# Second half of the tokens read transposed from memory, ScalarE copying operands of VectorE's sums to PSUM, and the rms factor moved to position 111

## The chip, the cores and the metric

The kernel runs on one core of a Trainium2 chip. A core has a matrix engine (TensorE, PE in the profile), a vector engine (VectorE, DVE), a scalar engine (ScalarE, ACT), GpSimd (POOL) and SyncE (SP), which here only issues DMAs. They run side by side and wait for each other by semaphores. The metric is the time of one execution on the device, in microseconds (us), lower is better. Everything is fp32.

## The reference

For x of 2048 tokens by 512 features:

```python
xn = layernorm(x)                                  # no weights
s  = xn @ (weight * block_mask).T                  # 512 x 512, 32x32 blocks kept or zeroed
nx = xn * rsqrt(mean(xn**2) + eps) * ln_w
g, u = nx @ gate_w.T, nx @ up_w.T                  # 1792 x 512 each
ffn = (silu(g) * u) @ down_w.T                     # 512 x 1792
out = x + s * silu(ffn)
```

## The kernel before

**Layout.** Activations are held transposed: features over the 128 partitions, tokens along the free axis, in tiles of 512 tokens. There are four token tiles (t = 0 to 3) and four chunks of features (c = 0 to 3), so the transposed xn is sixteen tiles of 128 x 512. Tokens 0 to 1023 (t = 0, 1) are the first half, t = 2, 3 the second.

**Fewer products.** Both levels of every matrix product use a scheme with seven block products in place of eight. It needs sums and differences of the operands' blocks. On the activations' side, the outer level (`outer_b`) makes four difference tiles (q = 5, 6, 7, 4) for each k and n out of blocks of both halves; the inner level (`inner_b`) makes four more (m = 5, 6, 7, 4) for each outer q. Outer blocks q = 1, 2 are tiles of the first half alone, 3 is the second half's own. The products run with q = 1 and 2 for all eight groups of weights first, and only then with q = 6, 5, 7, 3, 4, so that the second half has the first part of the run to be got ready.

**An order written out by hand.** The kernel calls no scheduler. `at(pos, fn)` records a step under a position, the steps are sorted by position, and this order is the order of each engine's queue. One position is one product of 128x128 with 128x512 on PE. An engine works strictly through its queue: an instruction that waits holds up all behind it. An instance j of seven products has its products at 7j, 7j+2, 7j+3, 7j+4, 7j+6, 7j+8 and 7j+12. Its "seed" at 7j+1 is a copy on ScalarE of the sum x so far into the bank z, which the product at 7j+3 then adds to; its "snapshots" s5 (7j+3) and s2 (7j+5) and its totals are on VectorE or ScalarE.

**PSUM.** Of eight banks, tag "V" has two, used in turn for transposes, for silu's results, for weights scaled on ScalarE and for small things. A third use waits until the first is read.

**The steps that the change touches.**

- `load_x` loads token-major x. `stats` takes mean and variance by token on VectorE, `factors` makes scale and bias from them (with a square root on ScalarE), `normalise` applies these on VectorE or ScalarE, `transpose` turns 128x128 blocks by PE (L155), and `evacuate` copies the banks to SBUF on ScalarE (L163). In the second half the blocks of c = 0 and 1 are not copied: VectorE's outer sums 5 and 7 read them from the bank (positions 51.5 to 74).
- `outer_b` 5, 6, 7 run on VectorE, 4 on GpSimd; `inner_b` 5, 6 on VectorE, 7, 4 on GpSimd. All go through the helper `add`, L97 in the profile.
- `rms_factor` makes the per-token rms factor at 36.2 to 37.4; `rms_store` (position 120) transposes it and stores it to memory, from where it is broadcast over the partitions near the end.
- GpSimd also makes the weights' sums (`inner_a`, also L97), at positions 7 below the instance that uses them.
- `x_t` is the transposed x in memory, read before only at the end, for the residual.

Of the kernel before, what the change touches and what calls it, by code (L numbers as in the profile page):

```python
# [8 lines left out]
F32 = mybir.dt.float32  # L9
I32 = mybir.dt.int32  # L10
AF = mybir.ActivationFunctionType
ALU = mybir.AluOpType
AX = mybir.AxisListType

P = 128
W = 512
# [15 lines left out]
def tile_masked_linear_gated_ffn(  # L32
# [11 lines left out]
    nc = tc.nc  # L44
    NT, H = x.shape
    KC = H // P
    G = gu.shape[0]
    NTT = NT // W
    TT = W // P
# [2 lines left out]
    h_dram = tc.dram_tile([7, G, 2, P, W], F32, name="h_dram")  # L52
    s_dram = tc.dram_tile([KC, NTT, P, W], F32, name="s_dram")
    rms_dram = tc.dram_tile([NT], F32, name="rms_dram")
    acc_dram = tc.dram_tile([G + 1, P, 4, W], F32, name="acc_dram")
    dw_dram = tc.dram_tile([4, P, G, 256], F32, name="dw_dram")

    const = ctx.enter_context(tc.tile_pool(name="const", bufs=1))
    small = ctx.enter_context(tc.tile_pool(name="small", bufs=2))
# [8 lines left out]
    def at(pos, fn, *args):  # L68
        events.append((pos, len(events), fn, args))
# [5 lines left out]
    mem = big.tile([P, sum(n for _, n in RINGS), W], F32, tag="mem", name="mem")  # L75
# [5 lines left out]
    F = first_slot  # L81

    def slot(tag, name=None):
        i, n = ring[tag]
        ring[tag][0] += 1
        return mem[:, first_slot[tag] + i % n, :]
# [6 lines left out]
    def bank(tag, name):  # L93
        return ps.tile([P, W], F32, tag=tag, name=name, bufs=PSB[tag])

    def add(eng, o, a, b, op=ALU.add):
        eng.tensor_tensor(o, a, b, op)  # L97

    dve, pool, act = nc.vector, nc.gpsimd, nc.scalar
# [3 lines left out]
    ident = const.tile([P, P], F32, tag="ident", name="ident")  # L103
# [9 lines left out]

    xt, raw, stat = {}, {}, {}
    agg = small.tile([P, NTT, TT, 2], F32, tag="agg", name="agg", bufs=1)
    rms = small.tile([P, NTT, TT], F32, tag="rms", name="rms", bufs=1)

    def load_x(t):
# [9 lines left out]
    def factors(t):  # L128


        scl = small.tile([P, TT], F32, tag="scl", name=f"scl_{t}")
        nb = small.tile([P, TT], F32, tag="nb", name=f"nb_{t}")
        stat[t] = (scl, nb)

        def last():
            nc.vector.reciprocal(scl, scl)
            nc.vector.scalar_tensor_tensor(nb, agg[:, t, :, 0], -1.0, scl, ALU.mult, ALU.mult)

        return [lambda: nc.vector.tensor_scalar(scl, agg[:, t, :, 1], 1.0 + EPS, EPS * EPS, ALU.mult, ALU.add),
                lambda: nc.scalar.activation(scl, scl, AF.Sqrt), last]  # L140
# [9 lines left out]
    pt = {}  # L150
# [17 lines left out]
    def rms_factor():  # L168

        def first():  # L170
            nc.vector.tensor_scalar_add(rms, agg[:, :, :, 1], EPS)
            nc.vector.reciprocal(rms, rms)
            nc.vector.tensor_mul(rms, agg[:, :, :, 1], rms)
            nc.vector.tensor_scalar_add(rms, rms, EPS)
        return [first, lambda: nc.scalar.activation(rms, rms, AF.Sqrt)]

    def rms_store():

        b = bank("V", "rms_rows")
        nc.tensor.transpose(b[: NTT * TT, :P], rms.rearrange("p t i -> p (t i)"), ident)  # L180
        rows = small.tile([NTT * TT, P], F32, tag="rms_rows", name="rms_rows", bufs=1)
        nc.vector.tensor_copy(rows, b[: NTT * TT, :P])
        nc.sync.dma_start(rms_dram.rearrange("(i p) -> i p", p=P), rows)

# [4 lines left out]
        nc.sync.dma_start(rms_bc[t], rms_dram[t * W : (t + 1) * W].unsqueeze(0).to_broadcast([P, W]))  # L189


    bblk, bop = {}, {}

    def outer_b(q, k, n, eng):


        B = lambda K, H_: pt[2 + n, k] if (K, H_) == (0, 1) else raw[2 * K + k, 2 * H_ + n]
        if q in (1, 2, 3):
            bblk[q, k, n] = B(*{1: (0, 0), 2: (1, 0), 3: (1, 1)}[q])
            return  # L200
        o = mem[:, F["free"], :] if (q, k, n) == (4, 0, 1) else slot("tmp" if (k, n) == (0, 1) else f"B{q}")
        a, b = {
            5: lambda: (B(0, 1), B(0, 0)),
            6: lambda: (B(1, 1), bblk[5, k, n]),
            7: lambda: (B(1, 1), B(0, 1)),
            4: lambda: (B(1, 0), bblk[6, k, n]),
        }[q]()
        add(eng, o, a, b, ALU.subtract)
        bblk[q, k, n] = o

    def inner_b(q, m, eng):

        b11, b12, b21, b22 = (bblk.get((q, k, n)) for k in (0, 1) for n in (0, 1))
        if q in (1, 2):
            b11, b21, b22 = (raw.get((2 * (q - 1) + k, n)) for k, n in ((0, 0), (1, 0), (1, 1)))
        o = slot(f"B{q}", f"t{q}_{m}")
        if q in (1, 2):
            b12 = pt[1, 2 * (q - 1)]
            if m == 6:
                b22 = pt[1, 2 * (q - 1) + 1]  # L220
        a, b = {
            5: lambda: (b12, b11),
            6: lambda: (b22, bop[q, 5]),
            7: lambda: (b22, b12),
            4: lambda: (b21, bop[q, 6]),
        }[m]()
        add(eng, o, a, b, ALU.subtract)
        bop[q, m] = o

    def operand(q, m):  # L230
# [325 lines left out]
    fin, at_later = {}, []  # L556

    def load_final(R, Hh, i, slot_s, slot_x):
        r, n = divmod(i, 2)
        t, m = 2 * Hh + n, 2 * R + r  # L560
        fin[m, t] = mem[:, slot_s, :], mem[:, slot_x, :]
        nc.sync.dma_start(fin[m, t][0], s_dram[m, t])
        s_tile = fin[m, t][0]
        at_later.append(lambda: nc.gpsimd.tensor_tensor(s_tile, s_tile, rms_bc[t], ALU.mult))  # L564
        nc.sync.dma_start(fin[m, t][1], x_t[m * P : (m + 1) * P, t * W : (t + 1) * W])

    def finish(R, Hh, i, y, pos, eng, part=slice(0, W), source=None):
        r, n = divmod(i, 2)
# [108 lines left out]
    T = lambda us: (us - 14.0) / 0.86  # L677
# [17 lines left out]
    def plan(pos, step, todo):  # L695
        for i, fn in enumerate(todo):
            at(pos + step * i, fn)


    def warm(n, b):  # L700
        for _ in range(n):
            nc.tensor.matmul(b[:, :P], ident, ident, start=True, stop=True, skip_group_check=True)

    at(T(1.4), lambda: warm(26, bank("V", "idle")))
    for t, p, step in ((0, T(7.1), 0), (1, T(12.5), 0), (2, 36.0, 1.2), (3, 36.1, 1.2)):
        plan(p, step, factors(t))
    for i in range(TT):
        half = act if i < 2 else dve
# [16 lines left out]
    for q in (1, 2):  # L725
        for k in (0, 1):
            for n in (0, 1):
                at(8, outer_b, q, k, n, None)
    at(2.1, scale_a, 1, 0)
    at(5.2, scale_a, 1, 1)  # L730
    for i in range(TT):
        at(14.0 + 2.5 * i, stats, 2, i)
        at(25.0 + 3 * i, stats, 3, i)
        at((44.0, 51.0, 55.2, 58.2)[i], normalise, 2, i, act)
        at(40.5 + 2.4 * i, normalise, 3, i, dve)
    plan(36.2, 1.2, rms_factor())

    for t, p0 in ((3, 51.5), (2, 65.5)):
        n = t % 2
        for k, c in enumerate((2, 3, 0, 1)):  # L740
            for i in range(TT):
                at(p0 + 2 * k + 0.01 * i, transpose, t, c, i, "V")
            if c >= 2:
                at(p0 + 2 * k + 1.2, evacuate, t, c, act)
            else:
                at(p0 + 2 * k + 1.2, outer_b, 5, c, n, dve)
                at(p0 + 2 * k + 1.21, outer_b, 7, c, n, dve)
    for k in (0, 1):
        for n in (0, 1):
            at(72, outer_b, 3, k, n, None)  # L750
    for n, p0 in ((1, 60), (0, 74)):
        for k in (0, 1):
            at(p0 + 1.5 * k, outer_b, 6, k, n, dve)
            at(p0 + 2.2 + 1.7 * k + (16 if n == 1 else 4), outer_b, 4, k, n, pool)
    for q, p in ((6, 77), (5, 83), (4, 89), (7, 100), (3, 118)):
        for off, m, eng in ((0, 5, dve), (3, 6, dve), (5.5, 7, pool), (7.5, 4, pool)):
            at(p + off, inner_b, q, m, eng)


    todo = {}  # L760
    for g in range(G + 1):
        p, rest = 7 * where[g, 1], 7 * where[g, BLOCKS[0]]
# [27 lines left out]
    for i, (R, K) in enumerate(QUADS):  # L790
        at(50, load_mask, R, K)
        at(62 + 3.5 * i, mask_rows, R, K)
    at(79.5, mask_blocks)
    at(120, rms_store)
    for t in range(NTT):
        at(END + 13, rms_rows, t)
# [9 lines left out]
    def D(o):  # L806
        return lambda k: free[25 * o + k] if 25 * o + k < 25 * len(DOWN) else free[25 * o + k - 1] + 1
# [6 lines left out]
    for o, q in enumerate(DOWN):  # L814
# [24 lines left out]
        for k in range(4):  # L839
            pos = END + (-6, -4.8, 2, 4)[k] if o == 0 else D(o - 1)(10) + 2.5 * k  # L840
# [7 lines left out]
    for (R, Hh), pos in (((0, 0), [D(0)(16)] * 4), ((1, 1), [D(2)(8)] * 4),  # L848
                         ((0, 1), [D(4)(20), D(4)(24), D(5)(3), D(5)(7)]),
                         ((1, 0), [D(5)(18), D(5)(22), D(6)(1), D(6)(5)])):  # L850
        for i, p in zip((0, 3, 1, 2), pos):
            at(p, load_final, R, Hh, i, fin_slots[0][i], fin_slots[1][i])
            at(p + 9, lambda: at_later.pop(0)())
# [71 lines left out]
```

## Time and profile before

| what | value |
|---|---|
| time, median of 3 runs | 513.14 us (512.75 to 513.34) |
| the profiled execution: its own time, and the span in it | 513.17 us, 511.4 us |
| PE busy, instructions | 505.8 us, 1269 |
| of them transposes (L155) | 64 of 128x128 |
| VectorE busy | 380.4 us, 590 instructions |
| ScalarE busy | 182.6 us, 348 |
| GpSimd busy | 340.9 us, 283 |
| TensorE clock granted | 1.0 |
| table loads of ScalarE | 4 of 1283 ns |
| DMA | 121.59 MB, mean 238 GB/s |

A busy time is a sum over the span, and a share of it says nothing on which engine is waited for. A row of the timeline has the start, the duration, the engine, the line, the operation and the tiles written and read, then how many of them are merged, and in brackets how long the engine was idle ahead of it and for whom. A row of groups has busy time and mean duration, then idle time. Consecutive instructions of one engine overlap, so the step from one start to the next is shorter than the duration.

### The profile page before, as it was taken

How to read it: one execution, taken by the hardware profiler on the slowest of the kernel's cores; microseconds unless marked ns; L12 is line 12 of the kernel's file. 1: busy time of each engine (PE TensorE's matmuls, PEld its weight loads, DVE VectorE, ACT ScalarE, POOL GpSimd, SP SyncE). 2: the span in 40 equal slices, each digit the busy share in tenths (PEclk: the TensorE clock that was granted, in tenths of full speed). 3: DMA queues.
4: the chain of work that ended last, by engine and by line, in shares of the span. 5: the costliest groups of instructions: out<-in, count | busy, mean ns of one | idle time of the engine just before them, and what ended most of it. 6: DMA issues, size and time to landing. Idle time of an engine off the chain costs nothing. (4 is left out here: it accounts for less than half of the span.)

```text
span 511.4 us, 4943 instructions
## 1 busy us (share of the span) xinstructions
PE 505.8 (99%) x1269; PEld 231.8 (45%) x1269; DVE 380.4 (74%) x590; ACT 182.6 (36%) x348; POOL 340.9 (67%) x283
## 2 busy tenths in 40 slices
PE   8999999999999999999999999999999999999997
PEld 8444444444444444444444444444444444444444
DVE  6878689876977969699696978968747645367736
ACT  4656754633536353353634433330100101001111
POOL 5522224994795968869597789976662754739960
PEclk9999999999999999999999999999999999999999
DMA  8436636369159386785948667499997698476472
GB/s 289 164 132 238 247 133 227 135 236 350 48 219 348 147 302 228 238 289 208 338 166 294 209 239 254 169 332 383 357 339 270 204 374 327 146 252 216 151 229 83
DMA packets 60460, 121.59 MB, mean 238 GB/s; under 512 B 5760, under 2 KB 13328, under 8 KB 58384
## 3 DMA queue, kind: packets, MB, share of 16 engines
q1 hardware_dynamic: 60288, 121.27, 66.8%
q8 instruction: 10, 0.16, 0.1%
q14 instruction: 18, 0.15, 0.1%
q10 hardware_dynamic: 144, 0.00, 0.0%
HBM read 75.11 MB, written 46.15 MB: 237 GB/s over the span
## 5 line engine op out<-in xcount | busy, mean ns | idle before, releaser
L97 POOL TENSOR_TENSOR mem<-mem 128x512 f32<-128x512 f32 (+4 forms) x245 | 305.2, 1267 | 135.4 <-ACT mem L264 36.5
L343 PE MATMUL x<-mem 128*128 128x512 f32 x448 | 213.6, 595 | 0.2 <-DVE mem L97 0.2
L343 PEld LDWEIGHTS x<-mem 128*128 128x128 f32 x448 | 83.7, 190 | 107.3 <-issue 86.9
L97 DVE TENSOR_TENSOR mem<-x,mem 128x512 f32<-128x512 f32 x137 | 92.5, 684 | 42.0 <-PE x L343 41.1
L343 PE MATMUL y<-mem 128*128 128x512 f32 x224 | 114.5, 593 | 0.3 <-DVE mem L97 0.3
L97 DVE TENSOR_TENSOR mem<-mem 128x512 f32<-128x512 f32 (+3 forms) x60 | 74.7, 1252 | 7.8 <-PE dx L591 4.3
L591 PE MATMUL dx<-mem 128*128 128x512 f32 x174 | 78.3, 592 | 0.0
L97 DVE TENSOR_TENSOR mem<-y,mem 128x512 f32<-128x512 f32 x96 | 65.6, 684 | 9.8 <-PE y L343 8.5
L343 PEld LDWEIGHTS y<-mem 128*128 128x128 f32 x224 | 42.2, 190 | 53.0 <-issue 47.8
L350 ACT COPY z<-x 128x512 f32<-128x512 f32 x54 | 30.9, 573 | 97.9 <-PE x L343 92.2
L343 PE MATMUL z<-mem 128*128 128x512 f32 x112 | 57.3, 593 | 0.0
L591 PEld LDWEIGHTS dx<-mem 128*128 128x128 f32 x174 | 33.1, 190 | 41.6 <-issue 40.4
L591 PE MATMUL dy<-mem 128*128 128x512 f32 x98 | 44.5, 592 | 0.0
L409 ACT ACTIVATE gate<-mem 128x512 f32<-128x512 f32 x56 | 33.1, 601 | 25.3 <-DVE mem L97 20.9
L414 DVE TENSOR_TENSOR mem<-gate,mem 128x512 f32<-128x512 f32 x56 | 38.0, 681 | 5.1 <-POOL mem L97 4.3
L564 POOL TENSOR_TENSOR mem<-mem 128x512 f32<-128x512 f32 x16 | 25.0, 1570 | 15.3 <-DMA mem<-s_dram 15.2
L343 PEld LDWEIGHTS z<-mem 128*128 128x128 f32 x112 | 21.0, 190 | 24.9 <-issue 23.9
L574 ACT ACTIVATE silu<-mem 128x512 f32<-128x512 f32 x15 | 9.0, 602 | 64.6 <-DVE mem L97 48.3
L97 DVE TENSOR_TENSOR mem<-z,mem 128x512 f32<-128x512 f32 x41 | 28.0, 682 | 3.5 <-PE z L343 3.5
L591 PEld LDWEIGHTS dy<-mem 128*128 128x128 f32 x98 | 18.6, 190 | 23.4 <-issue 23.4
L97 DVE TENSOR_TENSOR mem<-dx,mem 128x512 f32<-128x512 f32 x16 | 11.0, 690 | 20.1 <-PE dx L591 20.1
L591 PE MATMUL dz<-mem 128*128 128x512 f32 x56 | 25.2, 592 | 0.0
(73 smaller groups left out, 289.2 us busy)
## 6 DMA issues: line engine op xcount, KB each, us to landing
h_dram<-mem SPq DMA_DIRECT2D x98, 256.0 KB, 2.1
mem<-h_dram SPq DMA_DIRECT2D x28, 768.0 KB, 6.2
mem<-in_gu SPq DMA_DIRECT2D x42, 256.0 KB, 3.7
acc_dram<-mem SPq DMA_DIRECT2D x8, 1024.0 KB, 4.2
mem<-acc_dram SPq DMA_DIRECT2D x8, 1024.0 KB, 6.7
mem<-in_x SPq DMA_DIRECT2D x16, 256.0 KB, 5.2
s_dram<-mem SPq DMA_DIRECT2D x16, 256.0 KB, 4.8
mem<-s_dram SPq DMA_DIRECT2D x16, 256.0 KB, 6.3
```

Of the source, the lines that this page charges most:

```text
L97: eng.tensor_tensor(o, a, b, op)
L343: nc.tensor.matmul(st[key], weights(g, q, m), operand(q, m), start=first and not (key == "z" and seeded), stop=True, skip_group_check=True)
L350: nc.scalar.copy(st["z"], st["x"])
L409: nc.scalar.activation(gate[key], t(), AF.Silu)
L414: nc.vector.tensor_mul(a(), gate[key], b())
L564: at_later.append(lambda: nc.gpsimd.tensor_tensor(s_tile, s_tile, rms_bc[t], ALU.mult))
L574: nc.scalar.activation(b[0][:, part], y[:, part] if source is None else source(), AF.Silu)
L591: nc.tensor.matmul(st[key], w(), b(), start=first and key != "z", stop=True, skip_group_check=True)
```

## The change

The second half is no longer normalised and transposed on the chip. `x_t` is laid out in memory in tiles of 128 x 512, and the eight tiles of t = 2, 3 are loaded from it (`load_xt`). Mean and variance still come from the token-major x. The factors of a token tile (scale and bias, 128 x 8) are transposed by PE, copied by ScalarE, stored to memory and read back as two tiles that hold the factor of each token in every partition (`fac_rows`). GpSimd multiplies the eight tiles by the scale and adds the bias to the four of c = 2, 3 (`scale_xt`); for c = 0, 1 the sums are rearranged so that the bias drops out or comes in through another block: 7 is taken first, then 6 from 7, 5 from 6, and 4 from 6. For n = 1 GpSimd makes 7, 6 and 4; for n = 0 VectorE makes 7, 6 and 5, and 5 for n = 1.

Where VectorE makes an outer sum, and for inner sums 5 and 6 of the outer blocks 6, 5 and 4, ScalarE copies one operand to a V bank 0.9 positions earlier (`hold`): fourteen copies of 128 x 512. The rms factor moves from 36.2 to 111.5, and the positions of the inner sums come forward: block 6 from 77 to 68, 5 from 83 to 75, 4 from 89 to 81, 7 from 100 to 96.

```diff
-        rows = small.tile([NTT * TT, P], F32, tag="rms_rows", name="rms_rows", bufs=1)
+        rows = small.tile([NTT * TT, P], F32, tag="rows", name="rms_rows")
...
+    def load_xt(t, c):
+        K, k, n = c // 2, c % 2, t % 2
+        v = mem[:, F["v5"] + 4 + 2 * n + k, :] if K == 0 else slot("tmp" if (k, n) == (0, 1) else "B3")
+        (u12 if K == 0 else raw)[(k, n) if K == 0 else (c, t)] = v
+        nc.sync.dma_start(v, x_t[c, t])
+
+    def fac_rows(t):
+        b = bank("V", f"fac_rows_{t}")
+        nc.tensor.transpose(b[: 2 * TT, :P], fac[:, t - 2].rearrange("p f i -> p (f i)"), ident)
+        rows = small.tile([2 * TT, P], F32, tag="rows", name=f"fac_sb_{t}")
+        nc.scalar.copy(rows, b[: 2 * TT, :P])
+        nc.sync.dma_start(fac_dram[t - 2].rearrange("f (i p) -> (f i) p", p=P), rows)
+        for f in range(2):
+            fac_bc[t, f] = mem[:, F["B6"] + 3 + 2 * (t - 2) + f, :]
+            nc.sync.dma_start(fac_bc[t, f], fac_dram[t - 2, f].unsqueeze(0).to_broadcast([P, W]))
+
+    def scale_xt(t, c, f):
+        v = u12[c, t % 2] if c < 2 else raw[c, t]
+        add(pool, v, v, fac_bc[t, f], (ALU.mult, ALU.add)[f])
...
-            5: lambda: (B(0, 1), B(0, 0)),
-            6: lambda: (B(1, 1), bblk[5, k, n]),
-            7: lambda: (B(1, 1), B(0, 1)),
-            4: lambda: (B(1, 0), bblk[6, k, n]),
+            7: lambda: (B(1, 1), u12[k, n], ALU.subtract),
+            6: lambda: (bblk[7, k, n], B(0, 0), ALU.add),
+            5: lambda: (B(1, 1), bblk[6, k, n], ALU.subtract),
+            4: lambda: (B(1, 0), bblk[6, k, n], ALU.subtract),
...
+    def hold(key, v):
+
+        held[key] = bank("V", "held_" + "_".join(map(str, key)))
+        nc.scalar.copy(held[key], v())
+
+    def outer_b_held(pos, lag, q, k, n):
+        v = {7: lambda: u12[k, n], 6: lambda: raw[k, n], 5: lambda: raw[2 + k, 2 + n]}[q]
+        at(pos - lag, hold, (q, k, n), v)
+        at(pos, outer_b, q, k, n, dve)
+
+    def inner_b_held(pos, lag, q, m):
+        at(pos - lag, hold, (q, m), lambda: bblk[q, *{5: (0, 1), 6: (1, 1)}[m]])
+        at(pos, inner_b, q, m, dve)
...
-    for t, p, step in ((0, T(7.1), 0), (1, T(12.5), 0), (2, 36.0, 1.2), (3, 36.1, 1.2)):
+    for t, p, step in ((0, T(7.1), 0), (1, T(12.5), 0), (3, 22.6, 0.6), (2, 33.4, 1.2)):
...
-        at(14.0 + 2.5 * i, stats, 2, i)
-        at(25.0 + 3 * i, stats, 3, i)
-        at((44.0, 51.0, 55.2, 58.2)[i], normalise, 2, i, act)
-        at(40.5 + 2.4 * i, normalise, 3, i, dve)
-    plan(36.2, 1.2, rms_factor())
-
-    for t, p0 in ((3, 51.5), (2, 65.5)):
...
+        at(14.0 + 2.5 * i, stats, 3, i)
+        at(23.5 + 2.8 * i, stats, 2, i)
+    plan(111.5, 1.2, rms_factor())
+
+    for k, (t, c) in enumerate((t, c) for t in (3, 2) for c in (0, 2, 1, 3)):
+        at(21.0 + 1.5 * k, load_xt, t, c)
+    at(25.2, fac_rows, 3)
+    at(40.8, fac_rows, 2)
+    for n, p0 in ((1, 31), (0, 50)):
+        t = 2 + n
+        for off, c, f in ((0, 0, 0), (1.5, 2, 0), (3, 1, 0), (4.5, 3, 0), (9, 2, 1), (10.5, 3, 1)):
+            at(p0 + off, scale_xt, t, c, f)
+    for k in (0, 1):
+        at(37 + 1.5 * k, outer_b, 7, k, 1, pool)
+        at(43 + 1.5 * k, outer_b, 6, k, 1, pool)
+        at(61 + k, outer_b, 4, k, 1, pool)
+        at(67 + 1.3 * k, outer_b, 4, k, 0, pool)
+    for pos, lag, q, k, n in ((51.0, 0.9, 5, 0, 1), (53.0, 0.9, 5, 1, 1), (57.2, 0.9, 7, 0, 0), (58.5, 0.9, 6, 0, 0), (60.3, 0.9, 7, 1, 0),
+                              (61.4, 0.9, 6, 1, 0), (64.2, 0.9, 5, 0, 0), (65.6, 0.9, 5, 1, 0)):
+        outer_b_held(pos, lag, q, k, n)
...
-    for q, p in ((6, 77), (5, 83), (4, 89), (7, 100), (3, 118)):
-        for off, m, eng in ((0, 5, dve), (3, 6, dve), (5.5, 7, pool), (7.5, 4, pool)):
-            at(p + off, inner_b, q, m, eng)
+    for q, p in ((6, 68), (5, 75), (4, 81), (7, 96), (3, 118)):
+        for off, m in ((0, 5), (3, 6)):
+            if q in (7, 3):
+                at(p + off, inner_b, q, m, dve)
+            else:
+                inner_b_held(p + off, 0.9, q, m)
+        for off, m in ((5.5, 7), (7.5, 4)):
+            at(p + off, inner_b, q, m, pool)
```

More of the change, by code (lines that the diff above doesn't have):

```diff
@@ L54, in tile_masked_linear_gated_ffn @@
     rms_dram = tc.dram_tile([NT], F32, name="rms_dram")
+    fac_dram = tc.dram_tile([2, 2, W], F32, name="fac_dram")
     acc_dram = tc.dram_tile([G + 1, P, 4, W], F32, name="acc_dram")
@@ L115, in tile_masked_linear_gated_ffn @@
     agg = small.tile([P, NTT, TT, 2], F32, tag="agg", name="agg", bufs=1)
+    fac = small.tile([P, 2, 2, TT], F32, tag="fac", name="fac", bufs=1)
     rms = small.tile([P, NTT, TT], F32, tag="rms", name="rms", bufs=1)
@@ L128, in factors @@
     def factors(t):
-        scl = small.tile([P, TT], F32, tag="scl", name=f"scl_{t}")
-        nb = small.tile([P, TT], F32, tag="nb", name=f"nb_{t}")
+        if t < 2:
+            scl = small.tile([P, TT], F32, tag="scl", name=f"scl_{t}")
+            nb = small.tile([P, TT], F32, tag="nb", name=f"nb_{t}")
+        else:
+            scl, nb = fac[:, t - 2, 0, :], fac[:, t - 2, 1, :]
         stat[t] = (scl, nb)
@@ L189, in rms_rows @@
         nc.sync.dma_start(rms_bc[t], rms_dram[t * W : (t + 1) * W].unsqueeze(0).to_broadcast([P, W]))
+    u12, fac_bc = {}, {}
+    def load_xt(t, c):
[15 more added lines that the diff above has]
+        add(pool, v, v, fac_bc[t, f], (ALU.mult, ALU.add)[f])
     bblk, bop = {}, {}
     def outer_b(q, k, n, eng):
-        B = lambda K, H_: pt[2 + n, k] if (K, H_) == (0, 1) else raw[2 * K + k, 2 * H_ + n]
+        B = lambda K, H_: raw[2 * K + k, 2 * H_ + n]
         if q in (1, 2, 3):
@@ L201, in outer_b @@
         o = mem[:, F["free"], :] if (q, k, n) == (4, 0, 1) else slot("tmp" if (k, n) == (0, 1) else f"B{q}")
-        a, b = {
-            5: lambda: (B(0, 1), B(0, 0)),
-            6: lambda: (B(1, 1), bblk[5, k, n]),
-            7: lambda: (B(1, 1), B(0, 1)),
-            4: lambda: (B(1, 0), bblk[6, k, n]),
+        a, b, op = {
+            7: lambda: (B(1, 1), u12[k, n], ALU.subtract),
+            6: lambda: (bblk[7, k, n], B(0, 0), ALU.add),
+            5: lambda: (B(1, 1), bblk[6, k, n], ALU.subtract),
+            4: lambda: (B(1, 0), bblk[6, k, n], ALU.subtract),
         }[q]()
-        add(eng, o, a, b, ALU.subtract)
+        if (q, k, n) in held:
+            a, b = {7: (a, held[q, k, n]), 6: (a, held[q, k, n]), 5: (held[q, k, n], b)}[q]
+        add(eng, o, a, b, op)
         bblk[q, k, n] = o
+    held = {}
+    def hold(key, v):
[8 more added lines that the diff above has]
+        at(pos, inner_b, q, m, dve)
     def inner_b(q, m, eng):
@@ L226, in inner_b @@
         }[m]()
-        add(eng, o, a, b, ALU.subtract)
+        add(eng, o, held.get((q, m), a), b, ALU.subtract)
         bop[q, m] = o
@@ L564, in load_final @@
         at_later.append(lambda: nc.gpsimd.tensor_tensor(s_tile, s_tile, rms_bc[t], ALU.mult))
-        nc.sync.dma_start(fin[m, t][1], x_t[m * P : (m + 1) * P, t * W : (t + 1) * W])
+        nc.sync.dma_start(fin[m, t][1], x_t[m, t])
     def finish(R, Hh, i, y, pos, eng, part=slice(0, W), source=None):
@@ L731, in tile_masked_linear_gated_ffn @@
     for i in range(TT):
-        at(14.0 + 2.5 * i, stats, 2, i)
-        at(25.0 + 3 * i, stats, 3, i)
-        at((44.0, 51.0, 55.2, 58.2)[i], normalise, 2, i, act)
-        at(40.5 + 2.4 * i, normalise, 3, i, dve)
-    plan(36.2, 1.2, rms_factor())
-    for t, p0 in ((3, 51.5), (2, 65.5)):
[L739 to L747, printed above, removed]
+        at(14.0 + 2.5 * i, stats, 3, i)
@@ L748, in tile_masked_linear_gated_ffn @@
+    for pos, lag, q, k, n in ((51.0, 0.9, 5, 0, 1), (53.0, 0.9, 5, 1, 1), (57.2, 0.9, 7, 0, 0), (58.5, 0.9, 6, 0, 0), (60.3, 0.9, 7, 1, 0),
+                              (61.4, 0.9, 6, 1, 0), (64.2, 0.9, 5, 0, 0), (65.6, 0.9, 5, 1, 0)):
+        outer_b_held(pos, lag, q, k, n)
     for k in (0, 1):
         for n in (0, 1):
[L750 to L754, printed above, removed]
@@ L755, in tile_masked_linear_gated_ffn @@
-    for q, p in ((6, 77), (5, 83), (4, 89), (7, 100), (3, 118)):
-        for off, m, eng in ((0, 5, dve), (3, 6, dve), (5.5, 7, pool), (7.5, 4, pool)):
-            at(p + off, inner_b, q, m, eng)
+            at(73, outer_b, 3, k, n, None)
+    for q, p in ((6, 68), (5, 75), (4, 81), (7, 96), (3, 118)):
+        for off, m in ((0, 5), (3, 6)):
+            if q in (7, 3):
+                at(p + off, inner_b, q, m, dve)
+            else:
+                inner_b_held(p + off, 0.9, q, m)
+        for off, m in ((5.5, 7), (7.5, 4)):
+            at(p + off, inner_b, q, m, pool)
@@ L904 @@
         "x": x.reshape(B * S, H),
-        "x_t": x.reshape(B * S, H).T,
+        "x_t": x.reshape(-1, W, KC, P).transpose(2, 0, 3, 1),
         "ln_w": a("L0_ffn_ln_w").reshape(KC, P).T,
```

## The prediction

> **What bounds the kernel now.** I read the page from the busy times to the chain that ended last, then the waits of the matrix engine.
>
> ```profile
> PE 505.8 (99%) x1269; PEld 231.8 (45%) x1269; DVE 380.4 (74%) x590; ACT 182.6 (36%) x348; POOL 340.9 (67%) x283
> ...
> PE 35%; DVE 2%; POOL 1%; issue 0%; ACT 0%; DVEq 0%; POOLq 0%
> ```
>
> The waits of PE alone, over the whole span:
>
> ```profile
> PE idle L702 <- POOL ident masks.py:199: 1.3, 1, 1.3
> PE y L343 <- DVE mem L97: 0.3, 1, 0.3
> PE x L343 <- DVE mem L97: 0.2, 1, 0.2
> ```
>
> PE stands still for 1.8 us in 511.4. The program is a row of matmuls without a gap, so the time is the number of PE instructions times their pitch; VectorE, ScalarE and GpSimd only have to be in time. An instruction leaving PE is worth its pitch, and anything late at PE is paid in full.
>
> The pitch is in the timeline of PE, as difference of starts (the ends overlap):
>
> ```profile
> 56.89 1.02 PE L343 MATMUL y<-mem 128*128 128x512 f32 x2
> 57.74 0.60 PE L155 MATMUL pt<-ident,mem 128*128 128x128 f32 x4
> 58.18 1.02 PE L343 MATMUL z<-mem 128*128 128x512 f32 x2
> 59.04 1.02 PE L343 MATMUL x<-mem 128*128 128x512 f32 x2
> 59.90 0.60 PE L155 MATMUL pt<-ident,mem 128*128 128x128 f32 x4
> 60.34 1.02 PE L343 MATMUL x<-mem 128*128 128x512 f32 x2
> ```
>
> A product (two MATMULs) takes 0.86 us, which is one "position" of the kernel's program: position p starts near 13.1 + 0.8586 p us (17 at 27.70, 45 at 51.74), before the transposes. Four transposes take 0.44 us (58.18 - 57.74, 60.34 - 59.90), 0.11 each, not the 0.60 of the busy column.
>
> ScalarE, around the square roots:
>
> ```profile
> 41.64 0.58 ACT L361 COPY mem<-x 128x512 f32<-128x512 f32 x1 [0.33 <-PE x L343]
> 42.12 0.59 ACT L371 COPY mem<-z 128x512 f32<-128x512 f32 x1
> 42.59 0.62 ACT L409 ACTIVATE gate<-mem 128x512 f32<-128x512 f32 x1
> 43.13 0.90 ACT L264 ACTIVATE mem<-mem,lnw_sb 128x256 f32<-128x256 f32 x2
> 44.27 0.57 ACT L350 COPY z<-x 128x512 f32<-128x512 f32 x1 [0.24 <-PE x L343]
> 44.85 1.28 ACT L140 ACT_TABLE_LOAD   x1
> 46.15 0.30 ACT L140 ACTIVATE scl<-scl 128x4 f32<-128x4 f32 x2
> ```
>
> Here are ScalarE's pitches: 0.48 us for a copy, 0.54 for a silu, 0.8 for a scaled pair. The L350 copy is the "seed": it ends at 44.84 and PE's z product, which waits for it, starts at 45.73. So seeds have 0.89 to 0.95 us to spare, the smallest slack that repeats. VectorE's snapshots s5 and s2 have up to 1.68.
>
> GpSimd and VectorE between 56 and 86 us, and VectorE between 85 and 100, by form:
>
> ```profile
> L97 POOL TENSOR_TENSOR mem<-mem 128x256 f32<-128x256 f32 x10 | 7.2, 728 | 30.9 <-ACT mem L264 20.5 <-PE x L343 9.9
> L97 POOL TENSOR_TENSOR mem<-mem 128x512 f32<-128x512 f32 x1 | 1.3, 1269 | 0.0
> ```
>
> ```profile
> L97 DVE TENSOR_TENSOR mem<-pt,mem 128x512 f32<-128x512 f32 x4 | 2.7, 680 | 0.0
> ```
>
> ```profile
> L97 DVE TENSOR_TENSOR mem<-mem 128x512 f32<-128x512 f32 x5 | 4.7, 941 | 0.0
> ```
>
> GpSimd is nearly idle in the stretch that gets its new work.
>
> [...]two SBUF inputs cost 0.94 us on average where GpSimd runs, a PSUM operand keeps 0.68. So the copies to PSUM should keep the new GpSimd work from slowing VectorE. [...]The trace shows 1.28 and the square root 0.02 us behind it; [...]so I take 1.28[...]. [...]Stores of h_dram in a quiet queue land after 2.0 here, loads of in_gu after 2.6 to 2.8.
>
> **The change on PE.** It removes 32 transposes of the second half: eight groups of four, whose starts in the timeline take 0.44, 0.44, 0.43, 0.44, 0.43, 0.44, 0.44, 0.43, together -3.49 us. It adds two transposes of the factors: 2 x 0.11 = +0.22, by the 0.11 that the rms transpose takes (119.85 to 119.96). Products and their order stay. Against 513.17 this alone gives 509.90. The rest is what arrives late.
>
> **The factor broadcast (positions 25 to 35).** ScalarE copies the factors at about 36.0 us; SP stores them, waits for the landing (2.0 in a quiet queue; DMA is idle from 33 to 37 us), then issues B6.5's and B6.6's loads (2.7): usable at 41 us. Bounds: 2.0 + 2.6, and 4.0 + 6.1, what the rms store and the slowest rms broadcast took in busy queues. Queued behind SP's wait are four more x_t loads, two h stores and the acc store; their buffers are due some 10 us later, so they cost nothing. GpSimd then has three multiplications (1.23 pitch) until 44.7 and waits for ScalarE's scaled pair at about 45.8. So 1.1 us of lateness is free. From there it has work without a gap: per half six scalings and outer sums at 1.23, with the weight sums (0.72) between. I get 57.2 us for the last sum of the odd tile; its first user is at 57.9. The even tile's scalings end at 59.1, 61.8, 63.8, 65.0; their users come at 61.7, 62.4, 64.9, 65.7. Just in time, no cost. The weight sums keep over 2 us before their products.
>
> **Table loads.** The square root at 23.2 finds its table still loaded. The one at 34.6 needs a load between the silu at 33.5 and the seed at 36. Chain from the copy at 41.64: 0.48 + 0.47 + 0.63 (the load starts when the silu has ended) + 1.30 + 0.10 + 0.80 + 0.57 gives 45.99, and with the one factor transpose in front 46.10. PE's z is due at 45.73 + 0.11 = 45.84, and waiting adds 0.15 (as behind VectorE at 21.55). z starts at about 46.26: +0.42. The square root at 112.7 costs 1.4 us ahead of the seed at 113, of which over 1.1 is idle time: seed slack falls to 0.8, no cost. The silu at 26.2 starts 2.5 us later behind the factors' copy; its products delay VectorE's total at 30 from 39.8 to 41.1, due at 41.55: no cost. The four small VectorE operations of rms (1.1 us) fall at 111.5 beside slack of 1.68.
>
> **ScalarE and VectorE, positions 57 to 71.** ScalarE loses four normalisations (0.7) and four evacuations (0.48) and gets fourteen holds (0.48). From seed 57 (time 0) it has: seed 0.20, silu 0.68, hold 1.22, snap s5 1.92 (waits for PE), hold 2.56 (waits for VectorE to free its bank), scaled pair 3.04, hold 3.84, snap s2 4.32, total 4.80, silu 5.27, pair 5.81, hold 6.61, seed 64 at 7.09 instead of 6.21. It ends at 7.66, z is due at 7.73: on the edge. VectorE in the same time, each 0.60: held up by the hold at 60.5 until 4.46, then sum 6, mask row, total 62, total 63, h_out, sum 5 (from 7.46), total 65, mask row, second sum 5, snap 66 from 9.86 to 10.54. PE's y at position 69 wants that snapshot at 10.30: with 0.15, +0.39. Behind it the s2 for position 71 ends at 12.34, due at 12.41 after that shift: +0.08. From 73 on both engines catch up. At 50 to 56 the sums behind holds delay the totals by 0.8 of 1.68: nothing.
>
> **Positions 96 to 103.** Inner sum 5 of block 7 goes ahead of a snapshot, and six more sums (0.60) stand before the total that PE wants at 103: 0.5 left. [...]Bounds 0 and 0.4; I take 0.1. VectorE's sums elsewhere and the contiguous x_t of the final loads are hidden behind PE, which waits for no DMA at the end.
>
> **Sum.** 513.17 - 3.49 + 0.22 + 0.42 + 0.39 + 0.08 + 0.10 = 510.89, say 510.9. The profiled execution (span 511.4, 1.8 around it) is 0.03 over the median of 513.14, which I neglect. About 0.2% (1.03 us) is what this kernel's measurement can tell from no change; "faster" is below 512.11.
>
> **Rivals.** (a) All cover holds, PE loses the transposes and no more: 509.9. For it: the slack figures; against it: the table load chain, which I can't make fit. 18%. (b) The hold chains lock more tightly than I count: each hold waits for VectorE to free one of two V banks, and VectorE for the hold. With another 1.2 us of stalls between 57 and 80: 512.1. For it: ScalarE has 6.9 us of work in 6.0 there. 17%. (c) Slower: the broadcast through DRAM comes late. Every microsecond after 42.1 moves GpSimd's unbroken row; from about 43.5 VectorE's outer sums wait and hold back the totals behind them, some 1 us for each. Gains of 3.27 - 0.99 are left, so above 45.8 the kernel is slower, and with 47 and a hold queue behind it 514.3. For it: 4.0 and 6.1 in busy queues; against it: the idle DMA queue at 36 us. 7%. (d) [...]512.3; 5%. Mine: 53%.
>
> **Numbers.** Range 509.8 to 512.4: (a), mine with its stalls between 0.3 and 1.6, (b), (d). Below 512.11: (a), mine, more than half of (b), a part of (d): 0.83. Slower by 0.2%: most of (c): 0.06. Between: 0.11.
>
> **What would show it.** PE matmuls fall by 30. PE waits: one near 46 us on ScalarE's z, one near 72 on VectorE, each below 0.6; none on GpSimd. Table loads rise from four to six, 1.28 each. B6.5 lands near 41 us. VectorE's held sums take 0.68. I am wrong if PE waits more than 2.5 us in sum between 40 and 110 us, or if a scaling on GpSimd waits for fac_dram beyond 43.

## The result and the profile after

The changed kernel takes 510.87 us (median of 5 runs, 510.74 to 511.10) against 513.14 (512.75 to 513.39) of the kernel before, run beside it: ratio 0.9956, 95% interval 0.9941 to 0.997. The difference, 2.27 us or 0.44%, is above the 0.2% that can be told from no change. The profiled execution took 510.88 us, with a span of 509.1.

The page's first row, and then the waits of PE over the whole span:

```profile
PE 502.8 (99%) x1239; PEld 227.1 (45%) x1239; DVE 376.4 (74%) x582; ACT 187.0 (37%) x358; POOL 358.8 (70%) x299
```

```profile
PE idle L749 <- POOL ident masks.py:199: 1.3, 1, 1.3
PE y L390 <- DVE mem L98: 0.3, 1, 0.3
PE x L390 <- issue: 0.2, 1, 0.2
PE z L390 <- ACT z L397: 0.2, 1, 0.2
```

PE has 30 instructions fewer. The first two waits are those of before; the last is new, and so is the one of 0.2 us in the start-up with no releaser shown. The wait of x for VectorE, at 326 us in before, is no longer listed, but that product is still as late (0.31 us): its idle time in the records is 0.14 us where it was 0.15. This view misses most of what the change lost, because the records of two products overlap (1.02 us long at a step of 0.86): a product that starts 0.1 us late still starts before the modelled end of the one ahead of it. What is late is read from the starts. I put the start of each product in the trace of after beside that of the same product in the trace of before, and wrote down where the difference changes:

| position | what happens there | change of the difference, us |
|---|---|---|
| up to 2 | start-up | -0.21 |
| 26, 41 | transposes of the factors | +0.11, +0.11 |
| 38, 39 | z waits for its seed behind the square root's table | +0.34, +0.10 |
| 52 to 72 | 32 transposes gone | 8 x -0.44 |
| 66, 67 | z waits for its seed behind a hold | +0.13, +0.10 |
| 69, 70 | y waits for VectorE's snapshot | +0.13, +0.11 |
| 72 | x at 71 starts in time but takes longer, so the product behind it is late | +0.08 |
| 73 to the end | | +0.05 in sum |

From 66 on a transposes' group and a late product can fall on one step; there the table gives what is left over 0.44. The sum without the start-up is -2.3 us, and so is the difference of the medians. The start-up is no effect of the change: the product of position 2 started between 16.70 and 17.62 us in the traces of the kernels below, which are alike up to there.

The table load. ScalarE and then PE near position 38, timelines of after:

```profile
42.50 0.62 ACT L456 ACTIVATE gate<-mem 128x512 f32<-128x512 f32 x1
43.15 1.28 ACT L145 ACT_TABLE_LOAD   x1
44.44 0.20 ACT L145 ACTIVATE fac<-fac 128x4 f32<-128x4 f32 x1
44.55 0.89 ACT L311 ACTIVATE mem<-mem,lnw_sb 128x256 f32<-128x256 f32 x2
45.35 0.57 ACT L397 COPY z<-x 128x512 f32<-128x512 f32 x1
```

```profile
44.78 1.02 PE L390 MATMUL y<-mem 128*128 128x512 f32 x2
45.98 1.13 PE L390 MATMUL z<-mem 128*128 128x512 f32 x2 [0.18 <-ACT z L397]
46.94 1.45 PE L390 MATMUL x<-mem 128*128 128x512 f32 x3
```

The seed (L397) ends at 45.92 and z starts at 45.98. From y to z PE takes 1.20 us in place of 0.86: 0.34 late. The view calls 0.18 of it idle. And the product that was waited for takes 1.13 in place of 1.02, so the next one comes another 0.10 later (0.96 between starts).

Positions 64 to 70. PE, ScalarE and VectorE in timelines of after:

```profile
69.37 1.02 PE L390 MATMUL y<-mem 128*128 128x512 f32 x2
70.35 1.12 PE L390 MATMUL z<-mem 128*128 128x512 f32 x2
71.31 1.88 PE L390 MATMUL x<-mem 128*128 128x512 f32 x4
73.16 1.12 PE L390 MATMUL y<-mem 128*128 128x512 f32 x2
```

```profile
68.44 0.90 ACT L311 ACTIVATE mem<-mem,lnw_sb 128x256 f32<-128x256 f32 x2
69.23 0.58 ACT L247 COPY held<-mem 128x512 f32<-128x512 f32 x1
69.75 0.55 ACT L397 COPY z<-x 128x512 f32<-128x512 f32 x1
```

```profile
70.64 0.68 DVE L98 TENSOR_TENSOR mem<-x,mem 128x512 f32<-128x512 f32 x1
71.24 0.67 DVE L347 TENSOR_REDUCE mask_sums<-mem 128x16 f32<-128x512 int32 x1
71.83 0.68 DVE L98 TENSOR_TENSOR mem<-held,mem 128x512 f32<-128x512 f32 x1
72.43 0.68 DVE L98 TENSOR_TENSOR mem<-y,mem 128x512 f32<-128x512 f32 x1
```

The hold at 69.23 stands ahead of the seed at 69.75, and z at 70.35 starts 0.05 behind the seed's end. VectorE runs without a gap; its last row here is the snapshot of position 66, ending at 73.11, and y starts at 73.16. A mask row (TENSOR_REDUCE) is in front of it. Neither late product has an idle time shown, yet both took 1.12 and moved everything behind them.

The broadcast through memory. SP's queue and GpSimd's first scaling in timelines of after, then the last row of the view of the factors' tile in memory:

```profile
35.81 0.35 SPq L211 DMA_DIRECT2D fac_dram<-fac_sb  x1
37.05 0.82 SPq L214 DMA_DIRECT2D mem<-fac_dram  x2
```

```profile
41.01 3.73 POOL L98 TENSOR_TENSOR mem<-mem 128x512 f32<-128x512 f32 x3 [6.57 <-DMA mem<-fac_dram]
45.52 14.77 POOL L98 TENSOR_TENSOR mem<-mem 128x256 f32<-128x256 f32 x15 [0.78 <-ACT mem L311]
```

```profile
DMA to landing us min/median/max: 3.8/4.4/5.2
```

SP issues the first load as soon as the store has landed, 1.24 us after the store's issue; the load lands at 40.88, 3.83 after its own. GpSimd starts at 41.01, and after three scalings it waits 0.78 for ScalarE's scaled pair, then works without a gap above 0.1 us until 65.9.

### The profile page after: what moved, and what is told of

Same layout as the page of the kernel before. It is cut to its first block, busy times and chain, and to the rows that moved or that the text cites. A ratio compares the mean times of both kernels' runs of the same rounds, so it can differ in the third digit from the quotient of the medians.

```text
span 509.1 us, 4929 instructions
## 1 busy us (share of the span) xinstructions
PE 502.8 (99%) x1239; PEld 227.1 (45%) x1239; DVE 376.4 (74%) x582; ACT 187.0 (37%) x358; POOL 358.8 (70%) x299
## 5 line engine op out<-in xcount | busy, mean ns | idle before, releaser
L98 POOL TENSOR_TENSOR mem<-mem 128x512 f32<-128x512 f32 (+4 forms) x261 | 322.2, 1258 | 116.3 <-ACT mem L418 32.3
L98 DVE TENSOR_TENSOR mem<-mem 128x1536 f32<-128x1536 f32 (+3 forms) x50 | 66.3, 1331 | 6.9 <-PE dx L638 4.4
L397 ACT COPY z<-x 128x512 f32<-128x512 f32 x54 | 30.9, 572 | 91.8 <-PE x L390 88.8
```

The costliest lines, as they stand in the source:

```text
L397: nc.scalar.copy(st["z"], st["x"])
```

## The experiments

All are edits of the kernel after, timed beside the kernel before (five runs where no number is given). The steps are differences of PE's starts against after, as in the table above. Where an edit is worth less than 1 us, the interval of its ratio overlaps with that of after, and the start-up alone scatters by 0.9 us between traces; what such an edit does is therefore read from the steps and not from the medians.

**1. The square root behind the seed.** Is the 0.44 at 38 the table load, or the new work of the other engines there?

```diff
-    for t, p, step in ((0, T(7.1), 0), (1, T(12.5), 0), (3, 22.6, 0.6), (2, 33.4, 1.2)):
+    for t, p, step in ((0, T(7.1), 0), (1, T(12.5), 0), (3, 22.6, 0.6)):
...
+    for p, fn in zip((33.4, 36.4, 38.6), factors(2)):
+        at(p, fn)
```

> The square root of tile 2's factors goes from 34.6 to 36.4, behind the seed at 36, the reciprocal from 35.8 to 38.6. Theory A (the table load ahead of the seed makes PE's z product at position 38 late): that stall of 0.44 us goes, 510.4 us, and PE doesn't wait for ScalarE near 46 us. Theory B (the seed is late for another reason, GpSimd's new row or the factor transpose in front): the wait stays, 510.9.

Measured: 510.49 us (510.02 to 510.95), ratio 0.995 (0.9938 to 0.9963). The steps at 38 and 39 are -0.34 and -0.10, and nothing else changes. ScalarE and PE in timelines of this run:

```profile
44.25 0.57 ACT L397 COPY z<-x 128x512 f32<-128x512 f32 x1 [0.24 <-PE x L390]
44.84 1.28 ACT L145 ACT_TABLE_LOAD   x1
```

```profile
44.86 1.02 PE L390 MATMUL y<-mem 128*128 128x512 f32 x2
45.72 1.02 PE L390 MATMUL z<-mem 128*128 128x512 f32 x2
```

Now the seed goes ahead of the load, z comes 0.86 behind y and takes 1.02. The load itself is still there, behind the seed: what cost was its place, not that there is one more.

**2. VectorE's row ahead of the snapshot.** Two edits, each of which takes one instruction from in front of the snapshot of position 66: the held sum (5,1,0), or the second row of mask sums.

```diff
-                              (61.4, 0.9, 6, 1, 0), (64.2, 0.9, 5, 0, 0), (65.6, 0.9, 5, 1, 0)):
+                              (61.4, 0.9, 6, 1, 0), (64.2, 0.9, 5, 0, 0), (66.3, 1.6, 5, 1, 0)):
```

> The second held sum 5 (k = 1, n = 0) goes from 65.6 to 66.3, so that VectorE's snapshot at 66 comes ahead of it; its hold stays at 64.7. Theory A (VectorE's queue is full from 67 to 77 us, the order of one sum only picks the product that waits): the wait at position 69 goes, the one at 71 grows from 0.08 to about 0.3, 510.8 to 510.9. Theory B (the order at 66 is the cause): 0.24 to 0.32 less, 510.6.

Measured: 511.09 (510.69 to 511.4), ratio 0.9961 (0.9949 to 0.9974). Steps -0.13 and -0.10 at 69 and 70, and +0.21 at 71: what is behind the snapshot has no more room, and the gain is given back two products later, as theory A had it. The steps come to -0.02; the median's +0.22 doesn't appear in them (this profiled execution started 0.56 later).

```diff
-        at(62 + 3.5 * i, mask_rows, R, K)
+        at((62, 68.5, 69, 72.5)[i], mask_rows, R, K)
```

> The second row of mask sums (0.60 of VectorE's queue) goes from 65.5 to 68.5, behind both snapshots, nothing else is moved. Theory A (a full queue on VectorE): the waits at 69 and 71 go both, 0.32 less, 510.55. Theory B (the order of the held sum against the snapshot, or the hold's own lateness): the sum is still ahead of the snapshot and only a part goes, 510.7 to 510.9.

Measured: 510.6 (510.21 to 511.06), ratio 0.9952 (0.994 to 0.9965). Steps -0.13 and -0.10 at 69 and 70, -0.08 at 72. The mask rows have no user until 79.5, so nothing comes back, as theory A had it. PE in the timeline of this run: y is 0.86 behind the last product of the row before, and takes 1.02.

```profile
71.37 1.88 PE L390 MATMUL x<-mem 128*128 128x512 f32 x4
73.09 1.02 PE L390 MATMUL y<-mem 128*128 128x512 f32 x2
```

**3. No holds.** The fourteen copies to PSUM go away, and VectorE's sums read two SBUF operands.

```diff
-        at(pos - lag, hold, (q, k, n), v)
...
-        at(pos - lag, hold, (q, m), lambda: bblk[q, *{5: (0, 1), 6: (1, 1)}[m]])
```

> All fourteen holds are left out; VectorE's sums read both operands from SBUF. Theory A (two SBUF operands contend with GpSimd's unbroken row between 46 and 76 us): these sums take 0.9 to 1.3 us instead of 0.68, VectorE falls behind by 3 to 5 us in all, PE waits for it by 2 us or more, 512.7 to 515. Theory B (the copies are not needed, VectorE has room, and ScalarE without them is never late): the wait at 66 goes, 510.6.

Measured: 512.49 (511.75 to 513.09, 21 runs), ratio 0.9986 (0.998 to 0.9993). Steps: -0.22 at 66 and 67, where the hold no longer stands ahead of the seed, then +0.57 at 68, +0.80 at 69, +0.12 at 71: a net loss of 1.27 us (the profiled execution has 0.9 more of start-up besides). The groups by form between 56 and 80 us, VectorE and GpSimd, first of after, then without holds (the last two columns of the head are the sum of busy time and the mean of one in ns):

```profile
L98 DVE TENSOR_TENSOR mem<-held,mem 128x512 f32<-128x512 f32 x7 | 4.8, 684 | 1.2 <-ACT held L247 1.2
```

```profile
L98 POOL TENSOR_TENSOR mem<-mem 128x512 f32<-128x512 f32 x13 | 16.3, 1278 | 0.7 <-DVE mem L98 0.7
```

```profile
L98 DVE TENSOR_TENSOR mem<-mem 128x512 f32<-128x512 f32 x10 | 10.2, 1021 | 0.6 <-POOL mem L98 0.6
```

```profile
L98 POOL TENSOR_TENSOR mem<-mem 128x512 f32<-128x512 f32 x12 | 17.9, 1512 | 0.6 <-DVE mem L98 0.6
```

Without holds both engines are slower: VectorE by 0.34 us for a sum, GpSimd by 0.23. With both operands in SBUF a sum of VectorE took 1021 ns and one of GpSimd beside it 1512; with one of VectorE's operands in PSUM it was 684 and 1278. The 0.68 of the prediction came from 56 to 86 us of before, where GpSimd was busy for 8.0 of 30 us. From 85 to 100 us it was busy for all 15, and beside the 941 ns on average of two SBUF operands the sums with a PSUM operand (x) took 684 there too:

```profile
L97 DVE TENSOR_TENSOR mem<-x,mem 128x512 f32<-128x512 f32 x6 | 4.1, 684 | 1.2 <-PE x L343 1.1
```

The holds take fourteen times 0.48 us of ScalarE, which cost 0.22 us at PE, and save 1.49: they pay, by less than the 2 us that I had put on them.

**4. The rms factor where it was.**

```diff
-    plan(111.5, 1.2, rms_factor())
+    plan(36.2, 1.2, rms_factor())
```

> The rms factor goes back from 111.5 to 36.2, all else stays. Theory A (its work is hidden in both places; at 36.2 it shares the table load of the factors' root, so four table loads instead of six): 510.9, within 0.15. Theory B (the move mattered: four small operations on VectorE at 36.2 delay its snapshot s5 at 38 or the factors, and PE waits): 0.3 to 1 us more, 511.2 to 511.9.

Measured: 511.96 (511.43 to 512.89, 8 runs), ratio 0.9974 (0.9964 to 0.9985). In the trace of this run x at position 40 is 0.34 late and 0.10 longer. PE's timeline:

```profile
47.74 1.02 PE L390 MATMUL x<-mem 128*128 128x512 f32 x2
48.94 1.12 PE L390 MATMUL x<-mem 128*128 128x512 f32 x2 [0.18 <-DVE mem L98]
```

Four small operations of VectorE (1.19, 0.64, 0.25 and 0.17 us in this trace) stand there ahead of the total of position 37, and x at 40 waits for its bank, which that total frees. The two long ones took 0.17 and 0.34 us in the kernel before; what made them longer here is not shown. So the move of rms spares 0.44 us against leaving it. The median's +1.09 is more than that. The profiled run has 0.79 of start-up besides, which shows where such a scatter can come from; how much of the median it explains stays open.

**5. The transposes back.** Four transposes of the identity ahead of the first product of each of the instances 12 to 19, into its bank; the products overwrite them.

```diff
+                if m == 1 and 12 <= j < 20:
+                    for i in range(4):
+                        nc.tensor.transpose(st[key][:, i * P : (i + 1) * P], ident, ident)
```

> 32 transposes of the identity are put in front of the first product of instances 12 to 19, four at each, into the bank which that product then overwrites. Theory A (a transpose costs PE its pitch of 0.11 us): 3.5 us more, 514.4. Theory B (the gain of the change came in part from elsewhere, and a transpose costs less or more than its pitch, for instance 0.15 with a break in the stream of products): outside 514.0 to 514.8.

Measured: 514.3 (513.92 to 514.94, 20 runs), ratio 1.0021 (1.0014 to 1.0027), 3.43 us above after. The trace has eight steps of +0.44, and -0.25 at positions 148 and 149, where a product that is late in the kernels before and after comes in time (see 7). A transpose costs its pitch of 0.11 us in both places, where it was taken away and where it was put back, and these 32 are the whole gain of the change.

**6. A late broadcast.** The factors' transpose, copy, store and loads of the odd tile 5.7 and 3 positions later.

```diff
-    at(25.2, fac_rows, 3)
+    at(30.9, fac_rows, 3)
```

> The transpose, copy, store and broadcast of tile 3's factors go from 25.2 to 30.9, 4.9 us later, so that the broadcast lands near 46 us instead of 40.9. Theory A (by the working of the slower rival: 0.8 us are free, then 2.3 us of margin before the held sum at 51, and each further microsecond is paid by the totals behind it): GpSimd's row moves by 4 us, PE waits 1 to 2.5 us in sum near 60 and 66 us, 512 to 513.5. Theory B (the later GpSimd work and its users have room, the broadcast is not critical): below 511.2.

Measured: 517.2 (516.95 to 517.75), ratio 1.0079 (1.0067 to 1.0092). The first load lands at 50.04. Both theories had expected less. PE's timeline around the first loss, and the windows view of the same run (length; busy time of PE, its weight loads, VectorE, ScalarE and GpSimd; the granted clock of PE; share and rate of DMA):

```profile
50.11 1.88 PE L390 MATMUL x<-mem 128*128 128x512 f32 x4
54.62 1.41 PE L390 MATMUL y<-mem 128*128 128x512 f32 x2 [2.63 <-POOL mem L98]
55.83 1.91 PE L390 MATMUL z<-mem 128*128 128x512 f32 x2
57.53 2.49 PE L390 MATMUL x<-mem 128*128 128x512 f32 x4
```

```profile
50.00:52.00 2.00, 1.99 (x5) 0.57 (x3) 0.69 (x1) 0.99 (x3) 1.83 (x2) 1.00 0.94 265
54.60:55.30 0.70, 0.68 (x2) 0.44 (x3) 0.00 (x0) 0.00 (x0) 0.70 (x1) 1.00 0.00 0
55.34:58.74 3.40, 3.40 (x5) 1.33 (x5) 0.00 (x0) 1.39 (x3) 3.40 (x5) 0.50 0.93 247
58.75:60.00 1.25, 1.25 (x4) 0.53 (x3) 0.00 (x0) 0.80 (x2) 1.25 (x2) 1.00 0.98 413
60.00:64.00 4.00, 4.00 (x11) 1.76 (x10) 1.98 (x3) 3.19 (x7) 4.00 (x5) 1.00 0.87 324
```

The y that waits is position 44; it needs a weight sum (`inner_a`) that stands on GpSimd behind three scalings and no outer sum. It is 2.80 late. From about 55.3 to 58.7 PE's clock is then granted at 0.50, and three products (y itself and the two behind it) lose 1.80 more (0.35, 0.85, 0.60). Half of 3.40 us is 1.70; the remaining 0.10 is what a product that waited takes longer at full clock too. Another 1.8 us fall at 54, 55 and 64 to 66. In sum the steps are 6.4 us, close to the medians' difference of 6.3. (The 6.9 us in the expectation below, and with them its 43.1, contain 0.5 of start-up.)

```diff
-    at(25.2, fac_rows, 3)
+    at(28.2, fac_rows, 3)
```

> The factors' transpose, copy, store and broadcast loads of the odd tile three positions later (25.2 to 28.2), that is 2.6 us, in the kernel after. From the run with 5.7 positions (B6.5 landed at 50.0, PE lost 6.9 us) theory A says that each microsecond of the landing beyond about 43.1 is lost whole, first at the product of position 44 that waits for GpSimd's weight sum: with a landing between 44 and 46, 0.9 to 2.9 us, 511.8 to 513.8 us. Rival (the outer sums pay first, as I had it: nothing before 45.8): 510.9 us, no wait of PE on GpSimd. If the landing is before 43.1 neither pays, and the free margin is at least that.

Measured: 512.7 (511.88 to 513.73, 21 runs), ratio 0.9992 (0.9986 to 0.9999). The first load lands at 44.77, 3.9 later than in after. Steps: -0.11 and +0.29 where the factors' transpose is moved (in its new place it starts 0.18 late), then +0.52 at 64, +0.07 at 65, +0.76 at 66. PE's timeline:

```profile
69.27 1.10 PE L390 MATMUL x<-mem 128*128 128x512 f32 x2 [0.35 <-ACT mem L408]
70.20 1.02 PE L390 MATMUL y<-mem 128*128 128x512 f32 x2
71.94 1.12 PE L390 MATMUL z<-mem 128*128 128x512 f32 x2 [0.72 <-ACT z L397]
```

The time is what the first theory said, the place isn't: the weight sum of position 44 ends 2.28 us before its product here. What is late is GpSimd's scalings at 51.5 and 54.5. VectorE's sums 7 wait for these (1.21 and 0.53 us in this trace), ScalarE's holds for the next sums wait for VectorE (1.28 and 0.29), and behind the holds stand a snapshot and the seed. The second theory had the place right (the outer sums first), but expected no loss there, which is wrong. So the outer sums pay first, with 1.35 us at a landing of 44.77, and the weight sums pay at a landing somewhere between that and 50.04.

**7. The repairs together.** First the square root behind the seed and the second mask row later, as in 1 and 2; then also the hold of sum (5,0,0) behind the seed of 64, with that sum behind the total of 65, and all four mask rows later.

> The third factors' square root behind the seed, and the mask rows behind the snapshot, both at once. Theory A (the two stalls lie at different places and are independent): the wait at positions 38 and 39 goes (0.44 us) and those at 69, 70 and 72 go (0.31): 510.87 - 0.75 = 510.1 us. Rival (slack that one edit frees is used up by the other, because both only move ScalarE's and VectorE's rows against PE): no more than the better of the two alone, 510.4 or above.

Measured: 510.28 (510.04 to 510.49), ratio 0.9943 (0.993 to 0.9957); steps -0.34, -0.10, -0.13, -0.11, -0.08, in sum -0.76. The two are independent.

```diff
...
-                              (61.4, 0.9, 6, 1, 0), (64.2, 0.9, 5, 0, 0), (65.6, 0.9, 5, 1, 0)):
+                              (61.4, 0.9, 6, 1, 0), (65.1, 1.0, 5, 0, 0), (65.6, 0.9, 5, 1, 0)):
...
-        at(62 + 3.5 * i, mask_rows, R, K)
+        at((68.5, 69, 72.5, 76.5)[i], mask_rows, R, K)
```

> As the run before it, and the hold of sum (5,0,0) goes behind the seed of position 64 (its sum from 64.2 to 65.1), with all four mask rows behind the snapshot. Theory A: z at position 66 also comes in time, 0.23 us more, and no wait of PE on ScalarE or VectorE is left between 40 and 75 us: 510.87 - 0.98 = 509.9 us, which is what the transposes alone would give. Rival (the sum that starts later behind its hold pushes the snapshot of position 66 past its time): 0.2 to 0.3 us come back at position 69, 510.1 us or more.

Measured: 510.02 (509.4 to 510.67), ratio 0.9938 (0.9926 to 0.9951). Steps -0.44 at 38 and 39, -0.23 at 66 and 67, -0.23 at 69 and 70, -0.08 at 72: the 0.98 expected. All waits of PE in this run:

```profile
PE idle L749 <- POOL ident masks.py:199: 1.3, 1, 1.3
PE pt L160 <- PE z L390: 0.4, 1, 0.4
PE y L390 <- DVE mem L98: 0.3, 1, 0.3
```

None of them is later than 30 us. But this view misses short waits, and the starts show more. In this run eight products between 140 and 325 us come 0.09 to 0.31 us late and are then 0.10 longer. The first of them is the second of the two products of this row of PE's timeline:

```profile
140.43 2.13 PE L390 MATMUL x<-mem 128*128 128x512 f32 x4
```

The row takes 2.13 us where 1.88 is usual. The eight lose 2.1 us in sum. They are late by nearly the same amounts in the kernels before and after, so they are no part of the change's effect; what most of them wait for stays open. This is the fastest kernel of the study by its median; its interval overlaps with that of after, and that it is faster rests on the steps of the trace.

## Why the prediction was right

The forecast was 510.9 us, the time is 510.87. The mechanism was right: PE's instructions by their pitch, less what comes late at the places named. That the sum is hit to 0.03 us is in part luck, for single terms are off by up to 0.23 us and cancel, and the start-up, which is no part of the forecast, scatters by more. And PE is "without a gap" only in the waits view: 2.1 us of late products (see 7) are in the kernels before and after alike, and so drop out of the difference. By its own terms:

- The transposes, -3.49: shown. They came as eight groups of 0.44, and putting 32 back cost eight times 0.44.
- The factors' transposes, +0.22: measured +0.11 twice.
- The table load ahead of the seed of 36, +0.42: measured 0.44, and the whole of it goes when the square root is moved. The load took 1.28 us, the square root starts 0.01 behind its end, and z and the product behind it lost 0.44 and no more, so rival (d), 512.3 us, falls. The load near 113 left no step at PE, as said.
- Positions 57 to 71, +0.47: measured 0.55, at the places named but with other sizes. The z at 66, "on the edge" and put at nothing, lost 0.23; the y at 69, put at 0.39, lost 0.24; the 0.08 behind it was right. I had the order of the queues right. The seed of 64 was put 0.07 ahead of its due time and ended 0.07 behind it (70.30, where z was due at 69.37 + 0.86), and with that the 0.15 that a wait adds came on top. In the trace of after this is about 0.05 between the release and the start, and 0.10 in the product itself. The wait on VectorE near 72, which I had looked for among the waits, shows in the starts alone.
- Positions 96 to 103, +0.10: measured 0. VectorE's two sums of SBUF operands there, at 96.69 and 100.88, took 0.68 each, and GpSimd, idle from 94.3, began a sum of 128x640 only at 101.05; this is the one mis-sized term without an experiment of its own.
- The broadcast, usable at 41.0: the first scaling started at 41.01, but by two errors that cancel. The store took 1.24 us, not 2.0, and the load 3.83, not 2.7.
- GpSimd's row: the last sum of the odd tile ended at 56.88 where I had 57.2, the even tile's first scalings at 58.80, 61.52, 63.44 and 64.67 where I had 59.1, 61.8, 63.8 and 65.0.
- Rival (c), each microsecond past 43.5 lost at the outer sums: for a landing at 44.77 this gives 1.3 us, and 1.35 was measured there, by the sums named. For 50.04 it gives 6.5 and 6.4 was measured, but that is luck: 2.8 were lost at a weight sum that the rival doesn't name, 1.8 behind it, nearly all by the clock, and only 1.8 at the later positions.
- Rivals (a) and (b): the late products that (a) denied are there, 0.99 us in sum; the 1.2 us more that (b) put between 57 and 80 are not.
- The move of the rms factor: I costed its new place (nothing, right) and gave it no credit for leaving the old one, where it would have cost 0.44. The sum isn't touched, since the kernel with the move was the one forecast.

## What to carry to other kernels

Where PE never idles, count PE instructions by their pitch (here 0.86 us a product, 0.11 a transpose) and then go through each engine's queue for the instruction that ends in front of the tightest consumer; two or three such places of 0.2 to 0.4 us were the whole difference between the plain count of transposes and the time. Look for late products in the starts and not among the waits, which showed 0.2 of 1.0 us, and nothing of another 2.1 us that after has in common with before. An instruction with a far due time (a mask row, a square root with its table load) that stood ahead of one with a near due time could be moved at no cost; a held sum moved behind a snapshot was not free, because its own user was near.

## What was not expected of the hardware

- A product that had to wait was itself about 0.1 us longer (1.10 to 1.13 in place of 1.02), when it came 0.13 us late as when it came 0.76 late. A short wait thus cost 0.1 more than the delay of the start.
- PE stood still for 2.63 us in one run, and 0.7 us after it had started again its granted clock fell to 0.50 for 3.4 us, which cost 1.7 us on top. In after, without the stall, it was 1.00 throughout from 46 to 60 us.
- A store of the 4 KB of factors landed within 1.24 us when DMA was nearly idle (share 0.02), below the 2.0 us that I had taken from the stores of h_dram, which are of 256 KB. Behind other transfers on SP it took up to 5.2: with the factors' step 5.7 positions (4.9 us) later the landing of the first load came 9.2 later.
